# Gates r and z of a graph as one 2 x 2 block product in seven multiplications

## The chip, the cores and the metric

The kernel runs on one NeuronCore of a Trainium2 chip. The core has five engines that each work off their own instruction queue and wait for one another by semaphores: TensorE (PE: matrix multiplications into PSUM; its weight loads, PEld, run beside them), VectorE (DVE), ScalarE (ACT), GpSimd (POOL) and SyncE (SP, which here only issues transfers). All data are float32. The metric is the time of the device in microseconds for one execution of the whole program, median of three runs: 2230.82 us (2230.2 to 2232.75).

## The reference

There are 64 graphs of 256 nodes with 256 features. Layer 0 normalizes the adjacency, multiplies it with the features and a weight and applies a layer norm to the residual sum. Layer 1 computes three things from its result x: a convolution branch `x_conv` (a pointwise convolution, then one with 17 taps along the nodes, with a residual), a message branch `x_nmp`, and a gated recurrent unit that joins them:

```python
x_in = jnp.concatenate([x_conv, x_nmp], axis=-1)
gi = x_in @ w_ih.T + b_ih
gh = x @ w_hh.T + b_hh
r = jax.nn.sigmoid(gi_r + gh_r)
z = jax.nn.sigmoid(gi_z + gh_z)
nn_ = jnp.tanh(gi_n + r * gh_n)
return (1.0 - z) * nn_ + z * x
```

A layer norm follows on x plus this. For r and z the three inputs (x, x_nmp and x_conv, 256 features each) enter one sum, so r and z of a graph are one product of a 256 x 768 matrix with a 768 x 512 matrix, plus a bias. The n gate needs its hidden and its input part apart.

## The kernel before

**Quarters.** The 64 graphs go in four quarters of Q = 16. A quarter passes three stages. *Layer graphs* (`graphs`, which runs `layer0` and `layer1`): per graph the adjacency is transposed, layer 0 computed, x and x_nmp transposed are written to DRAM (`xn_d`, 512 KB a graph), x itself to `x1_d`, and the first half of the convolution's transform goes into the large tile V. *Transform*: the convolution of the whole quarter as a Fourier transform over tiles of nodes: `products` multiplies 71 weight tiles `u` of 256 KB, streamed from DRAM through the ring `ustream`, and `real_transform`, `complex_begin` and `complex_end` do the inverse transform on VectorE, almost all of it with two inputs in SBUF; the result goes to `xc_d`. *Gates* (`gru`, one graph a call).

**How the stages are interleaved.** They are Python generators merged by hand. V shares its memory with the transform's results, so a quarter's graphs and the transform before it exclude one another, except that the first AHEAD = Q // 2 = 8 layer graphs of the next quarter write to a second tile, V2, during the transform; four ScalarE copies then bring V2 into V (L925). The first EARLY = 4 gate graphs of a quarter run among the remaining eight layer graphs of the next; the twelve `late` ones run during that next quarter's transform. A gate graph has four yields; the transform takes 14 of the 48 late yields between its product steps, and the others are merged with `complex_end` and with layer graphs. The last quarter has no graphs behind it: its 16 gate graphs run alone at the end.

**Order.** The tile framework derives all semaphores and gives each engine a fixed order of instructions. This isn't always the program's: an instruction whose buffer or data are there early may stand ahead of one that the program has first.

**A gate graph before.** For each half c of the nodes (128 of 256) TensorE runs six matmuls of 512 columns into one PSUM bank (L748: hidden, x_nmp and xcT terms), the bank `p_rz`, and six of 256 columns into another (L759, `p_n`). In the second half it transposes the convolution of the next graph (`transposed`, L726), from which ScalarE makes `xcT` with bias and ReLU (L728). VectorE adds the bias into `trz` (L763), ScalarE applies tanh with half the argument, which is a sigmoid up to scale (L764), GpSimd computes z3 = z + 3 (L766) and x1 * z3 (L767), VectorE does the n gate (L769, L770, L773), ScalarE its tanh (L776). Both halves done, VectorE joins them (L787, L788), and the layer norm follows: statistics on VectorE (L290 to L292), the power −0.5 on GpSimd (L293), scale on ScalarE (L303), transfer out (L790).

**Loads of the gates.** SP loads `x1_g` (L708), `xn_g` (L710) and the convolution `xc_g` (L704) into rings of two. `residual` (L715) adds x to `xc_g` by an accumulating transfer that GpSimd issues. PSUM has two rings of four banks: `bank` for transposes and layer graphs, `accbank` for products and gates.

**Degrees.** From the third graph on, ScalarE sums the rows of the adjacency with a copy into a tile called `unused` (L324), whose content nobody reads.

Of the kernel before, what the change touches and what calls it, by code (L numbers as in the profile page):

```python
# [9 lines left out]
F32 = mybir.dt.float32  # L10
# [4 lines left out]
P = 128  # L15
# [11 lines left out]
def kernel(  # L27
# [44 lines left out]

    ps = ctx.enter_context(tc.tile_pool(name="ps", bufs=4, space=bass.MemoryType.PSUM))
    psacc = ctx.enter_context(tc.tile_pool(name="psacc", bufs=4, space=bass.MemoryType.PSUM))
    loads = ctx.enter_context(tc.tile_pool(name="loads", bufs=3))
    work = ctx.enter_context(tc.tile_pool(name="work", bufs=2))
    freq = ctx.enter_context(tc.tile_pool(name="freq", bufs=1))
    small = ctx.enter_context(tc.tile_pool(name="small", bufs=4))
# [4 lines left out]
    def accbank(name):  # L83
        return psacc.tile([P, 512], F32, tag="acc", name=name)
# [30 lines left out]

    ident = const.tile([P, P], F32)
    make_identity(nc, ident)
    unused = const.tile([P, N], F32)
    neg_half = const.tile([P, 4], F32)
    nc.vector.memset(neg_half, -0.5)  # L120
    nc.vector.tensor_scalar(alpha_t, alpha_t, MIN_ALPHA, None, op0=ALU.max)
# [7 lines left out]
            nc.gpsimd.memset(t[:, :, c : c + 1], 1.0)  # L129
        scols.append(t)  # L130

    wih = const.tile([P, 2 * DCH, 3 * D], F32)
    whh = const.tile([P, DCH, 3 * D], F32)
    brz_t = const.tile([P, 2 * D], F32)
    bn_t = const.tile([P, 2, D], F32)

    bn2_bias = const.tile([P, DCH], F32)
# [176 lines left out]
    def layer0(g):  # L314

        a_t, x_t = ain.pop(g), xin.pop(g)


        deg = small.tile([P, NCH], F32, name="deg")
        if g < 2:  # L320
            nc.vector.tensor_reduce(deg, a_t, AX.X, ALU.add)
        else:
            for c in range(NCH):
                nc.scalar.activation(unused, a_t[:, c, :], AF.Copy, accum_out=deg[:, c : c + 1])  # L324
        nc.vector.scalar_tensor_tensor(deg, deg, 0.0, deg, op0=ALU.is_equal, op1=ALU.add)
        dis = small.tile([P, NCH], F32, name="dis")
        nc.gpsimd.tensor_tensor(dis, deg, neg_half[:, :NCH], op=ALU.pow)
# [2 lines left out]

        adjT = work.tile([P, NCH, 3, P], F32, name="adjT", bufs=3)
        ADJT[g] = adjT
        p = bank("p_adjT").rearrange("p (c n) -> p c n", c=NCH)
        for mc in range(NCH):
            for c in range(NCH):
# [239 lines left out]
    def turned(re, im, angle):  # L577


        t = freq.tile([P, 2, D], F32, name="turn", bufs=4)  # L580
        x, y = M[:, re, :], M[:, im, :]
        real_part(t[:, int(re > im), :], x, y, angle)
        return imaginary_part(t[:, int(re < im), :], x, y, angle), t
# [4 lines left out]
    def real_transform():  # L588


        sub2(M[:, 0:3:2, :], M[:, 1:4:2, :])
        yield

        sub2(M[:, 4:6, :].rearrange("p a o -> p (a o)"), M[:, 6:8, :].rearrange("p a o -> p (a o)"))
        add2(M[:, 6, :], M[:, 7, :])
        r = math.sqrt(0.5)
        for i, by in enumerate((-1.0, 1.0, -r, r)):
            stt(M[:, 4 + i, :], M[:, 4 + i, :], by, M[:, i, :], op0=ALU.mult, op1=ALU.add)
        stt(M[:, 0:4, :], M[:, 0:4, :], 2.0, M[:, 4:8, :], op0=ALU.mult, op1=ALU.subtract)
        yield  # L600

        four(8, 12)
        yield
        nc.vector.tensor_sub(M[:, 8, :], M[:, 0, :], M[:, 8, :])
        nc.vector.tensor_add(M[:, 12, :], M[:, 4, :], M[:, 12, :])
        for i, x, y in ((1, 9, 13), (2, 10, 14), (3, 15, 11)):
            angle = math.pi * ORDER[i] / 8
            t = freq.tile([P, 2, D], F32, name="turn", bufs=4)
            by = real_part(t[:, 0, :], M[:, x, :], M[:, y, :], angle)
            imaginary_part(t[:, 1, :], M[:, x, :], M[:, y, :], angle)  # L610
            stt(M[:, 8 + i, :], t[:, 0, :], -by, M[:, i, :], op0=ALU.mult, op1=ALU.add)
            stt(M[:, 12 + i, :], t[:, 1, :], by, M[:, 4 + i, :], op0=ALU.mult, op1=ALU.add)
            yield
        stt(M[:, 0:8, :], M[:, 0:8, :], 2.0, M[:, 8:16, :], op0=ALU.mult, op1=ALU.subtract)
        yield
# [39 lines left out]
    def output(q, n, re, im):  # L655


        plain = M[:, n // 8 * 8 + ORDER.index(n % 8), :]
        x, y = M[:, re, :], M[:, im, :]
        t = freq.tile([P, 2, D], F32, name="turn", bufs=4)  # L660
        by = [real_part(t[:, j, :], x, y, 2 * math.pi * (n + 16 * j) / FL) for j in range(2)]
        low = min(re, im)
        for j in range(2):
            stt(M[:, low + 16 * j, :], t[:, j, :], by[j], plain, op0=ALU.mult, op1=ALU.add)  # L664
        nc.sync.dma_start(
            xc_d[q].rearrange("g (t a b) d -> (g t) a b d", a=2, b=16)[:, :, n, :], M[:, low : low + 17 : 16, :]
        )
# [29 lines left out]
            yield  # L697


    GATE, CONV, XCT = {}, {}, {}  # L700

    def load_conv(g):
        CONV[g] = gate.tile([P, NCH, D], F32, name="xc_g")
        nc.sync.dma_start(CONV[g], xc_d[g // Q][g % Q].rearrange("(c p) d -> p c d", p=P))  # L704

    def load_gate(g):
        x1 = gate.tile([P, NCH, D], F32, name="x1_g")
        nc.sync.dma_start(x1, x1_d[g // Q][g % Q].rearrange("(c p) d -> p c d", p=P))  # L708
        xn = gate.tile([P, 2 * DCH, N], F32, name="xn_g")
        nc.sync.dma_start(xn, xn_d[g])  # L710
        GATE[g] = x1, xn

    def residual(g):

# [4 lines left out]
    def transposed(g):  # L719

        xc = CONV.pop(g)
        XCT[g] = gate.tile([P, DCH, N], F32, name="xcT")
        p = bank("p_xcT").rearrange("p (k n) -> p k n", k=DCH)
        for k in range(DCH):
            for c in range(NCH):
                nc.tensor.transpose(p[:, k, c * P : (c + 1) * P], xc[:, c, k * P : (k + 1) * P], ident)  # L726
        for k in range(DCH):
            nc.scalar.activation(XCT[g][:, k], p[:, k], AF.Relu, bias=bn2_bias[:, k : k + 1])  # L728

    def gru(g):  # L730

        following = g % Q + 1 < Q
        (x1, xn), xcT = GATE.pop(g), XCT.pop(g)
        trz = gate.tile([P, NCH, 2 * D], F32, name="trz", bufs=1)
        nn = gate.tile([P, NCH, D], F32, name="nn", bufs=1)
        if following:
            load_gate(g + 1)
        for c in range(NCH):
            cs = slice(c * P, (c + 1) * P)

            hid = [(xn[:, k, cs], whh[:, k, :]) for k in range(DCH)]
            inp = [(xn[:, DCH + k, cs], wih[:, DCH + k, :]) for k in range(DCH)]
            inp += [(xcT[:, k, cs], wih[:, k, :]) for k in range(DCH)]

            q = accbank("p_rz")
            terms = hid + inp
            for j, (lhsT, w) in enumerate(terms):
                nc.tensor.matmul(q, lhsT, w[:, : 2 * D], start=j == 0, stop=j == len(terms) - 1)  # L748
            if following and c == 1:
                transposed(g + 1)  # L750
            yield
            if following and c == 0:
                residual(g + 1)
            if c == 1 and g % Q + 2 < Q:
                load_conv(g + 2)
            p = accbank("p_n")
            for o, terms in ((1, hid), (0, inp)):
                for j, (lhsT, w) in enumerate(terms):
                    nc.tensor.matmul(  # L759
                        p[:, o * D : (o + 1) * D], lhsT, w[:, 2 * D :], start=j == 0, stop=j == len(terms) - 1  # L760
                    )

            nc.vector.tensor_add(trz[:, c, :], q, brz_t)  # L763
            nc.scalar.activation(trz[:, c, :], trz[:, c, :], AF.Tanh, scale=0.5)  # L764
            z3 = gate.tile([P, D], F32, name="z3", bufs=1)
            nc.gpsimd.tensor_scalar(z3, trz[:, c, D:], 3.0, None, op0=ALU.add)  # L766
            nc.gpsimd.tensor_tensor(x1[:, c, :], x1[:, c, :], z3, op=ALU.mult)  # L767
            gn = gate.tile([P, 2, D], F32, name="gn")
            nc.vector.tensor_add(gn, p.rearrange("p (i d) -> p i d", i=2), bn_t)  # L769
            nc.vector.scalar_tensor_tensor(  # L770
                gn[:, 1, :], trz[:, c, :D], 1.0, gn[:, 1, :], op0=ALU.add, op1=ALU.mult
            )
            nc.vector.scalar_tensor_tensor(  # L773
                gn[:, 0, :], gn[:, 1, :], 0.5, gn[:, 0, :], op0=ALU.mult, op1=ALU.add
# [8 lines left out]
            else:  # L783
                yield
                continue
            y, t, n = x1[:, part], trz[:, part, D:], nn[:, part]
            nc.vector.scalar_tensor_tensor(n, t, 1.0, n, op0=ALU.subtract, op1=ALU.mult)  # L787
            nc.vector.tensor_sub(y, y, n)  # L788
            layernorm(y, nc.scalar, 4 * LN_EPS)
# [48 lines left out]
    with tc.tile_pool(name="setup", bufs=1) as setup:  # L838
# [8 lines left out]
        load(2)  # L847

        def gate_weights():
            nc.sync.dma_start(whh, w_hhT.rearrange("(k p) o -> p k o", p=P))  # L850
            nc.sync.dma_start(wih, w_ihT.rearrange("(k p) o -> p k o", p=P))
            yield

        others = [weights(setup, i, Q, scale2) for i in range(Q)]
        others[4] = chain(others[4], gate_weights())
        run(graphs(0, range(Q), V, others))
        bih_t = setup.tile([P, 3 * D], F32, name="bih", tag="taps", bufs=2)
        nc.sync.dma_start(bih_t, bcast_rows(b_ih, 3 * D))
        bhh_t = setup.tile([P, 3 * D], F32, name="bhh", tag="taps", bufs=2)
        nc.sync.dma_start(bhh_t, bcast_rows(b_hh, 3 * D))  # L860
        nc.vector.tensor_add(brz_t, bih_t[:, : 2 * D], bhh_t[:, : 2 * D])
        nc.vector.tensor_copy(bn_t[:, 0, :], bih_t[:, 2 * D :])
        nc.vector.tensor_copy(bn_t[:, 1, :], bhh_t[:, 2 * D :])
    ustream = ctx.enter_context(tc.tile_pool(name="ustream", bufs=6))
    gate = ctx.enter_context(tc.tile_pool(name="gate", bufs=2))
    ahead = ctx.enter_context(tc.tile_pool(name="ahead", bufs=1))


    AHEAD = Q // 2
    V2 = ahead.tile([P, FL, DCH, AHEAD * GT], F32, name="V2")  # L870
    EARLY = 4

    def gates(q, part):

        for i in part:
            if i == 0:
# [4 lines left out]
                residual(q * Q)  # L881
                yield
                transposed(q * Q)
                yield
            yield from gru(q * Q + i)

# [99 lines left out]
```

## Time and profile before

| what | value |
|---|---|
| median of three runs | 2230.82 us (2230.2 to 2232.75) |
| profiled execution | 2229.6 us |
| its span, first to last instruction | 2227.7 us |
| TensorE clock granted, mean | 0.993 |
| VectorE, ScalarE, GpSimd busy | 1347.2, 839.9, 611.9 us |
| L748, three groups of 512 records | 243.2, 243.0, 241.3 us busy |
| L759, three groups of 512 records | 133.2, 131.7, 131.4 us busy |
| last transform: first product, last store to `xc_d` | 1708.0, 1913.5 us |

A logical float32 matmul shows as two records. The busy mean of a TensorE record (593 ns for 512 columns) overlaps its neighbours, since matmuls are pipelined; the distance from one to the next is the price, and the chain of waits gives it. Busy times of the other engines are of single instructions, which also overlap a little when they follow one another without a wait. Where a line gives a releaser ("<-ACT trz L764 649.9"), the engine sat idle that long until the named instruction was done.

### The profile page before, as it was taken

What the parts mean: (1) busy time and instruction counts of PE and PEld (TensorE: products, weight loads), DVE (VectorE), ACT (ScalarE), POOL (GpSimd) and SP (SyncE); (2) the same over time, 40 slices, a digit from 0 to 9 for tenths busy, and PEclk for the clock granted to TensorE, in tenths of its full rate; (3) what the DMA queues carried; (4) which work ended last, traced back from release to release, by engine and by line L of the source; (5) the groups of instructions that cost most, each with busy time, mean ns of one, the idle gap of its engine ahead of it and who ended that gap; (6) DMA issues with size and microseconds to landing.
All of it is one profiled execution on the core that took longest, in us unless ns stands there. A gap on an engine that the chain in (4) does not pass through costs nothing. (4 is left out here: it accounts for less than half of the span.)

```text
span 2227.7 us, 26520 instructions
## 1 busy us (share of the span) xinstructions
PE 2140.2 (96%) x8701; PEld 1533.4 (69%) x8701; DVE 1347.2 (60%) x3487; ACT 839.9 (38%) x1850; POOL 611.9 (27%) x656
## 2 busy tenths in 40 slices
PE   5999989999999999999999999999999999999998
PEld 4777768777767766777667766777776765556555
DVE  6555558895447796545446779545444779644444
ACT  3565633456431124446441122555532112222222
POOL 2344320113211133222221133222221114433332
PEclk9999999999999999999999999999999999999999
DMA  4655667444346644333236655333324655433331
GB/s 121 199 173 158 182 219 235 156 144 125 105 128 194 187 136 136 113 95 111 79 102 181 196 165 146 100 109 109 100 76 128 198 157 141 124 100 99 100 99 52
DMA packets 249732, 305.03 MB, mean 137 GB/s; under 512 B 18458, under 2 KB 227626, under 8 KB 249595
## 3 DMA queue, kind: packets, MB, share of 16 engines
q1 hardware_dynamic: 181500, 199.85, 29.2%
q10 hardware_dynamic: 45280, 68.04, 8.4%
q0 software_dynamic: 22816, 35.45, 8.3%
q8 instruction: 69, 1.13, 0.2%
q14 instruction: 67, 0.55, 0.1%
HBM read 200.71 MB, written 102.57 MB: 136 GB/s over the span
## 5 line engine op out<-in xcount | busy, mean ns | idle before, releaser
L766 POOL TENSOR_SCALAR z<-trz 128x256 f32<-128x256 f32 x128 | 125.0, 977 | 649.9 <-ACT trz L764 649.9
L748 PE MATMUL p_rz<-wih,xcT 128*128 128x512 f32 x512 | 241.3, 593 | 2.2 <-ACT xcT L728 2.2
L748 PE MATMUL p_rz<-wih,xn_g 128*128 128x512 f32 x512 | 243.2, 594 | 0.0
L748 PE MATMUL p_rz<-whh,xn_g 128*128 128x512 f32 x512 | 243.0, 594 | 0.0
L293 POOL TENSOR_TENSOR ln_rs<-ln_rs,neg_half 128x2 f32<-128x2 f32 x129 | 99.0, 767 | 428.9 <-DVE ln_rs L292 371.7
L763 DVE TENSOR_TENSOR trz<-p_rz,brz_t 128x512 f32<-128x512 f32 x128 | 87.7, 686 | 164.5 <-PE p_rz L748 164.4
L776 ACT ACTIVATE nn<-gn 128x256 f32<-128x256 f32 x128 | 53.3, 417 | 351.6 <-DVE gn L773 351.1
L748 PEld LDWEIGHTS p_rz<-wih,xcT 128*128 128x128 f32 x512 | 96.9, 190 | 124.0 <-issue 120.2
L748 PEld LDWEIGHTS p_rz<-wih,xn_g 128*128 128x128 f32 x512 | 96.2, 190 | 118.3 <-issue 118.2
L486 PE MATMUL p_k<-u,VM 128*128 128x256 f32 x736 | 175.2, 380 | 0.8 <-DMA u<-ud 0.7
L769 DVE TENSOR_TENSOR gn<-p_n,bn_t 128x512 f32<-128x512 f32 x128 | 88.1, 688 | 143.3 <-PE p_n L759 143.2
L486 PEld LDWEIGHTS p_k<-u,VM 128*128 128x128 f32 x736 | 138.3, 190 | 24.9 <-issue 4.6
L358 PE MATMUL p_hT<-adjT,x 128*128 128x256 f32 x512 | 126.9, 393 | 19.4 <-DVE adjT L341 11.9
L748 PEld LDWEIGHTS p_rz<-whh,xn_g 128*128 128x128 f32 x512 | 94.6, 190 | 64.8 <-issue 59.6
L303 ACT ACTIVATE x_g<-x_g,ln_mr,ln_rs 128x256 f32<-128x256 f32 x128 | 70.0, 593 | 181.4 <-DVE ln_mr L301 181.4
L764 ACT ACTIVATE trz<-trz 128x512 f32<-128x512 f32 x128 | 80.5, 629 | 152.8 <-DVE trz L763 108.3
L396 PE MATMUL p_conv<-wc,xn 128*128 128x259 f32 x512 | 126.9, 390 | 7.5 <-ACT xn L388 7.5
L759 PE MATMUL p_n<-whh,xn_g 128*128 128x256 f32 x512 | 133.2, 383 | 0.0
L759 PE MATMUL p_n<-wih,xn_g 128*128 128x256 f32 x512 | 131.7, 379 | 0.0
L759 PE MATMUL p_n<-wih,xcT 128*128 128x256 f32 x512 | 131.4, 379 | 0.0
L431 PE MATMUL p_dft<-fwd,h 128*128 128x240 f32 x512 | 117.9, 374 | 13.7 <-ACT h L400 13.3
L462 PE MATMUL p_nmp<-aT,msg 128*128 128x256 f32 x512 | 123.6, 385 | 5.9 <-DVE aT L457 5.9
(149 smaller groups left out, 4123.8 us busy)
## 6 DMA issues: line engine op xcount, KB each, us to landing
u<-ud SPq DMA_DIRECT2D x284, 256.0 KB
xn_d<-xn ACTq DMA_DIRECT2D x64, 512.0 KB
xn_g<-xn_d SPq DMA_DIRECT2D x64, 512.0 KB
adj_t<-in_adj_dram SPq DMA_DIRECT2D x64, 256.0 KB
x_t<-in_x_dram SPq DMA_DIRECT2D x64, 256.0 KB
x_d<-x ACTq DMA_DIRECT2D x64, 256.0 KB
x_g<-x_d SPq DMA_DIRECT2D x64, 256.0 KB
xc_d<-VM SPq DMA_DIRECT2D x64, 256.0 KB
```

Of the source, the lines that this page charges most:

```text
L293: nc.gpsimd.tensor_tensor(rs[:, : len(chunks)], rs[:, : len(chunks)], neg_half[:, : len(chunks)], op=ALU.pow)
L358: nc.tensor.matmul(p[:, k, :], x1[:, mc, k * P : (k + 1) * P], adjT[:, mc, 1 - mc : 3 - mc, :].rearrange("p n q -> p (n q)"), start=mc == ...
L396: nc.tensor.matmul(p, x1T[:, k, c * P : (c + 1) * P], wc1[:, k, :], start=k == 0, stop=k == DCH - 1)
L431: nc.tensor.matmul(p[:, t0 * FL : t1 * FL], h[:, c, k * P : (k + 1) * P], fwd[:, first : first + t1 - t0, :].rearrange("p t f -> p (t f)") ...
L462: nc.tensor.matmul(p[:, k, :], msg[:, mc, k * P : (k + 1) * P], aT[:, mc].rearrange("p n q -> p (n q)"), start=mc == 0, stop=mc == NCH - 1,)
L486: nc.tensor.matmul(p[:, j * D : (j + 1) * D], v[:, k, :], u[:, k, :], start=k == 0, stop=k == DCH - 1)
L748: nc.tensor.matmul(q, lhsT, w[:, : 2 * D], start=j == 0, stop=j == len(terms) - 1)
L759: nc.tensor.matmul(p[:, o * D : (o + 1) * D], lhsT, w[:, 2 * D :], start=j == 0, stop=j == len(terms) - 1)
L763: nc.vector.tensor_add(trz[:, c, :], q, brz_t)
L764: nc.scalar.activation(trz[:, c, :], trz[:, c, :], AF.Tanh, scale=0.5)
L766: nc.gpsimd.tensor_scalar(z3, trz[:, c, D:], 3.0, None, op0=ALU.add)
L769: nc.vector.tensor_add(gn, p.rearrange("p (i d) -> p i d", i=2), bn_t)
```

## The change

Write a graph's inputs, transposed and stacked (768 rows: x, x_nmp, xcT; HALF = 3 of its six row blocks each), as a 2 x 2 block matrix: the halves of the nodes against the halves of the inputs. The weights of r and z form one too: halves of the inputs against the columns of r and of z. The product of two such block matrices takes eight block products; in Strassen's form (Winograd's variant) it takes seven, with sums of blocks ahead and behind. The change does this:

- `gate_weights` loads three weight blocks and one for the sums (B11, B21, B22, T1), and makes the sums T1 to T4 by four VectorE subtractions, once. The weights of n get their own tile `wn`. It is now spread over graphs 4 to 6 of the first quarter.
- `input_sums` makes four sums of input blocks a graph, 128 x 384 each, on GpSimd, called for the next graph during a graph's n gate. x, x_nmp and xcT now share one tile, `inputs`.
- `gru` runs seven block products of three matmuls of 256 columns into four PSUM banks (the last half of one is empty), and five VectorE and GpSimd operations put r and z together: `first` (the first product plus bias), then `trz` in three VectorE additions that read PSUM, and one on GpSimd, 512 columns wide, that adds `first` to both z parts. The bias of z is stored less that of r. Two tanh of 512 columns follow, for r and for z. The transposes of the next graph come ahead of the n gate.
- Buffers: rings of loads 3 to 2, `turn` 4 to 3, `xc_g` 2 to 1, `ustream` 6 to 5, the tile `unused` goes (the copy of the degrees writes into `adjT`, which is filled later), V2 holds AHEAD = 6 graphs, and EARLY is 5, so that 44 late yields are left.

```diff
-    loads = ctx.enter_context(tc.tile_pool(name="loads", bufs=3))
+    loads = ctx.enter_context(tc.tile_pool(name="loads", bufs=2))
...
-                nc.scalar.activation(unused, a_t[:, c, :], AF.Copy, accum_out=deg[:, c : c + 1])
+                nc.scalar.activation(adjT[:, c, 0:2, :].rearrange("p n q -> p (n q)"), a_t[:, c, :], AF.Copy, accum_out=deg[:, c : c + 1])
...
-        CONV[g] = gate.tile([P, NCH, D], F32, name="xc_g")
+        CONV[g] = gate.tile([P, NCH, D], F32, name="xc_g", bufs=1)
...
+    def halves(inputs):
+
+        return [inputs[:, i * HALF : (i + 1) * HALF, c * P : (c + 1) * P] for c in range(2) for i in range(2)]
+
+    def input_sums(g):
+        A11, A12, A21, A22 = halves(GATE[g][1])
+        S = SUMS[g] = gate.tile([P, 4, HALF, P], F32, name="sums", bufs=1)
+        nc.gpsimd.tensor_tensor(S[:, 2], A11, A21, op=ALU.subtract)
+        nc.gpsimd.tensor_tensor(S[:, 0], A21, A22, op=ALU.add)
+        nc.gpsimd.tensor_tensor(S[:, 1], S[:, 0], A11, op=ALU.subtract)
+        nc.gpsimd.tensor_tensor(S[:, 3], A12, S[:, 1], op=ALU.subtract)
...
-            q = accbank("p_rz")
-            terms = hid + inp
-            for j, (lhsT, w) in enumerate(terms):
-                nc.tensor.matmul(q, lhsT, w[:, : 2 * D], start=j == 0, stop=j == len(terms) - 1)
-            if following and c == 1:
-                transposed(g + 1)
-            yield
-            if following and c == 0:
-                residual(g + 1)
...
+        def block(p, j, a, b):
+            for k in range(HALF):
+                nc.tensor.matmul(
+                    p[:, j * D : (j + 1) * D], a[:, k], wrz[:, b, k], start=k == 0, stop=k == HALF - 1
+                )
+
+        p15, p26 = accbank("p_rz"), accbank("p_rz")
+        block(p15, 0, A11, B11)
+        block(p26, 0, A12, B21)
+        block(p15, 1, S[:, 0], T1)
+        block(p26, 1, S[:, 1], T2)
+        yield
+        if following:
+            residual(g + 1)
+        first = gate.tile([P, 2, D], F32, name="first", bufs=1)
+        nc.vector.tensor_add(first, half(p15), brz_t)
+        nc.vector.tensor_add(trz[:, 0:2], first[:, 0:1].to_broadcast([P, 2, D]), half(p26))
+        p7, p34 = accbank("p_rz"), accbank("p_rz")
+        block(p7, 0, S[:, 2], T3)
+        block(p34, 0, S[:, 3], B22)
+        block(p34, 1, A22, T4)
+        nc.vector.tensor_add(trz[:, 3], trz[:, 1], p7[:, :D])
+        nc.vector.tensor_add(trz[:, 1:3], trz[:, 1:4:2], half(p34))
+        nc.gpsimd.tensor_tensor(
+            trz[:, 1:4:2], trz[:, 1:4:2], first[:, 1:2].to_broadcast([P, 2, D]), op=ALU.add
+        )
+
+        for i in range(2):
+            nc.scalar.activation(trz[:, i:4:2], trz[:, i:4:2], AF.Tanh, scale=0.5)
+        if following:
+            transposed(g + 1)
+        yield
         for c in range(NCH):
...
+            if c == 0 and following:
+                input_sums(g + 1)
             if c == 1 and g % Q + 2 < Q:
                 load_conv(g + 2)
...
-            nc.vector.tensor_add(trz[:, c, :], q, brz_t)
-            nc.scalar.activation(trz[:, c, :], trz[:, c, :], AF.Tanh, scale=0.5)
...
-    ustream = ctx.enter_context(tc.tile_pool(name="ustream", bufs=6))
+    ustream = ctx.enter_context(tc.tile_pool(name="ustream", bufs=5))
...
-    AHEAD = Q // 2
+    AHEAD = 6
...
-    EARLY = 4
+    EARLY = 5
```

## The prediction

> **What bounds the kernel now.** I read the page's busy shares first, then the groups of instructions, then the chain that ended last, then busy times by stretch, then single instructions on GpSimd. The shares:
>
> ```profile
> PE 2140.2 (96%) x8701; PEld 1533.4 (69%) x8701; DVE 1347.2 (60%) x3487; ACT 839.9 (38%) x1850; POOL 611.9 (27%) x656
> PE   5999989999999999999999999999999999999998
> ```
>
> TensorE is busy in every slice after the first. The chain of waits prices the gates (windowed to 1800–1970 us; columns: start, length, piece):
>
> ```profile
> 1909.25 5.15 PE p_rz L748 x12
> 1914.40 0.44 PE p_xcT L726 x4
> 1914.84 2.59 PE p_n L759 x12
> 1917.43 5.15 PE p_rz L748 x12
> ```
>
> Twelve 128x512 records take 5.15 us (0.429 each), twelve 128x256 records 2.59 us (0.2158 each): time goes with the columns, and a narrow matmul loses nothing although each has its own weight load. A logical matmul is two records. A gate graph is 2 x (5.15 + 2.59) + 0.44 = 15.92 us, and the pure gate stretch at the end repeats at exactly that. The stretches:
>
> ```profile
> 400.00:502.00 102.00, 94.98 (x441) 73.05 (x439) 90.22 (x257) 51.85 (x117) 17.47 (x17) 1.00 0.45 145
> 1298.00:1386.00 88.00, 87.68 (x303) 54.13 (x301) 83.63 (x211) 22.69 (x50) 30.27 (x28) 1.00 0.49 140
> 1825.00:1914.00 89.00, 86.81 (x283) 51.50 (x282) 83.42 (x199) 18.07 (x37) 38.65 (x27) 1.00 0.45 127
> 1965.00:2220.00 255.00, 254.46 (x830) 151.65 (x828) 115.06 (x263) 63.27 (x129) 82.45 (x96) 1.00 0.35 92
> ```
>
> Columns after the length: busy us of PE, weight loads, DVE, ACT, POOL. In the last stretch (gates alone) only TensorE is full; DVE is at 45%, GpSimd at 32%. But where the inverse transform is merged with gates (1298–1386, 1825–1914, and 767–856 with 84.35 of 89), DVE is at 94–95%. Work taken from TensorE there is worth nothing once DVE is the longer one. GpSimd in such a stretch:
>
> ```profile
> 1888.92 2.57 POOL L766 TENSOR_SCALAR z<-trz 128x256 f32<-128x256 f32 x1 [7.08 <-ACT trz L764]
> 1891.58 3.87 POOL L767 TENSOR_TENSOR x_g<-x_g,z 128x256 f32<-128x256 f32 x1
> ```
>
> and over the whole run (ns, least/median/most):
>
> ```profile
> L351 POOL TENSOR_TENSOR x_t<-x_t,b_t x64: 1256/1268/1737, 11.9 to 1647.6; 128x512 f32<-128x512 f32 x64
> L767 POOL TENSOR_TENSOR x_g<-x_g,z x128: 713/727/3866, 528.2 to 2219.4; 128x256 f32<-128x256 f32 x128
> ```
>
> The same multiplication takes 0.73 us alone and up to 3.87 beside a full DVE.
>
> **What the Trainium skill says.** "GPSIMD Engine Reference", section 3.1: a two-input elementwise operation costs GpSimd about 2.6 cycles of 1.2 GHz an element (2.17 ns). The trace agrees: (1256 − 713)/256 = 2.12 ns, plus 0.17 us fixed. "SBUF — State Buffer", section "Who interferes with whom": a VectorE instruction with two SBUF inputs contends with a GpSimd instruction that reads SBUF, one input (the other in PSUM) does not. The trace agrees on the blocking: at 1891.58 the multiplication lasts 3.87 us beside two-input transform steps; at 1862.55 it runs in 0.72 and a transform step (L574) beside it takes 0.94 instead of 0.42. "Trainium Kernel Development and Optimization", "Key Constraints": GpSimd can't access PSUM; so DVE must do the additions that read products, and only one of the recombinations can go to GpSimd. No row here tests that.
>
> **The change part by part.**
>
> *TensorE, removed:* per graph 24 records of 512 columns, 10.30 us. *Added:* seven products of three matmuls, 42 records of 256 columns x 0.2158 = 9.06. Saving 1.24 us a graph, x 64 = **−79.2 us**. A gate graph becomes 14.68. Nothing else on TensorE changes in amount.
>
> *DVE, added:* per graph two L763 additions (0.69 each) become first, trz 0:2 and trz 1:3 at 512 columns and one at 256: 3 x 0.69 + 0.42 = 2.49 against 1.38; in back-to-back flow, where the timeline spaces 512-wide ones 0.60 and 256-wide ones 0.335 apart, 2.14 against 1.21. About +1 us a graph. In the last stretch DVE goes from 7.2 to 8.3 us of 14.68: hidden by the products.
>
> *GpSimd, added:* four sums of 384 columns, 0.17 + 384 x 0.00212 = 0.98 each, and the z addition of 512 columns, 1.26: +5.2 us a graph. Before: two z (0.855), two x_g (0.73), ln_rs 0.72, residual's transfer 1.26 = 5.15. After 10.3 of 14.68: not the bound by its sum. ACT: two tanh of 512 columns as before; the second waits for GpSimd.
>
> *The three merged stretches:* 44 records of each of three L748 kinds in 1825–1914, eight of each a graph, are 5.5 graphs. Ideal length 89 − 5.5 x 1.24 = 82. DVE would need 83.4 + 5.5 x 0.93 = 88.5, and each added GpSimd operation holds a two-input DVE step about 0.4 us (0.94 against 0.42 above; 0.83 against 0.42 at 1911.75): 27 x 0.4 = 11 at most, 99 in all. Between 89 and 99, some transform work sliding into later stretches that have room (in 1386–1542 DVE is at 78.5 of 156): I take 92, so 10 us back each, **+30** (bounds +15 to +50).
>
> *The moved graphs:* AHEAD 8 to 6. A layer graph is 12.2 us of TensorE: 32 records x 0.216, 8 of conv x 0.218, 8 of the transform x 0.2, 4 of dist x 0.216, 10 transposes x 0.11. In the first round there are no gates to fill with, and 400–502 has DVE at 90 of 102: moving two graphs out takes 24.4 us from TensorE but only about 13 from DVE (7.4 busy a graph, less overlap). I take half of the difference back, **+6** (0 to +12). In later rounds one gate graph moves from late to early: late 12 to 11 graphs. The last round's transform then has 11 x 14.68 us of gates as cover where it had 12 x 15.92, 30 us less; gates of the round begin at about 1965 while DVE ends the transform at 1914 and the reload, residual, transposes and sums take some 15 us: a slack of 36. Still hidden, with about 6 to spare; if DVE is 20 late, 14 are lost (inside the bound above).
>
> *Rings.* u 6 to 5: one buffer is four records, 0.86 us less lead; TensorE waited 5 us for u in all. loads 3 to 2: a load starts one graph later, still one layer graph (over 12 us) ahead. xc_g 2 to 1: the reload of g+2 starts after the transposes of g+1; 3 us reload (2058.14 to the residual's issue at 2061.32), 1.26 issue, 4.4 landing = 9 of 14.68. GpSimd's sums, z, x_g and ln_rs queue behind a residual that waits for a late reload; SP's other loads stand behind the reload's own wait. Together **+3** (0 to +15). Weight loads: as many bytes in more transfers, and four subtractions of 768 columns (0.95 each by the 512 and 1024 rows) in the first stage, DVE at 26 of 50: nothing; uncovered 4. Degrees written into adjT: its third buffer was last read a graph before: nothing; uncovered, 0.4 a graph. *Layer norms behind the sums:* ln_rs and dis queue on GpSimd behind up to 4 us of sums, and DVE's L301 waits in order, with transform and PSUM readings behind it: **+6** in the three graph stages, **+3** in the last stretch (0 to +25).
>
> Sum: −79.2 + 30 + 6 + 3 + 9 = −31. The profiled execution took 2229.6 us (span 2227.7 and 1.9 around it): 2198.4. The median of the runs is 1.2 higher: **2199.6**.
>
> **Rivals.** (1) *Near the full saving*: DVE's ending transform slides and GpSimd's waits stay local. For it: DVE averages 60%, TensorE's waits are a few us. Against: 94% in three stretches. −79 + 25 = −54 or better: 2150–2177. (2) *Slower, by a ring through GpSimd in gru.* In the program's order: z addition 1.26, tanh 0.63, two xcT 0.84, four sums 3.94, z and x_g twice with gaps 3.46, L788 to ln_rs 2.1 (timeline), ln_rs 0.72, residual 1.26, hand-offs 0.4: 14.6 us, as long as TensorE's 14.68. It decides from 15.92: with the mean excess of z and x_g over quiet (0.977 and 0.878 against 0.855 and 0.727, about 0.14) on eleven operations it is 16.1: the 47.5 graphs outside the merged stretches lose 0.2 each, 10 us. Inside, the means are 1.57 and 1.72, 0.85 in excess; if half of the eleven meet it, the ring is 19.3, and 16.5 graphs lose 3.4 each, 56 us. Doubled inputs and x1 let TensorE run a graph ahead of the ring, so I take half of the 66: 2264 (2240 to 2297). Against it: the queue isn't in program order (a residual at 2061.32 stands ahead of the ln_rs at 2065.68 of a graph before), S, z3 and the additions only need their own data. (3) *No net change*: the merged stretches become DVE's, 3 x 18, and the ring costs 25: 2231.
>
> **How the numbers follow.** Two runs differ by up to 0.1%, so 0.2% (4.5 us) is about what tells from no change. Partial saving (2177–2218) 0.38, near full 0.20, about nothing (2218–2240) 0.10, slower 0.32, nearly all the ring. Faster: 0.58 and 0.03 of the third: 0.61; same 0.06; slower 0.33. Range 2158 to 2260: it leaves 0.06 below and 0.14 above; the likeliest case alone is 2177–2218.
>
> **What would show it.** 42 p_rz records a graph, 256 columns each and 0.216 apart; the last stretch at 14.7 a graph; no TensorE wait on the sums tile. DVE at 97% in the merged stretches, GpSimd near 945 us busy plus blocking. Wrong if TensorE waits for sums, xc_g or p_rz readings in the last stretch, or if the DVE-full stretches grow by more than 10 us each.

## The result and the profile after

The changed kernel takes 2328.7 us (median of four runs, 2323.78 to 2333.23) against 2231.78 for the kernel before beside it: ratio 1.0434, interval 1.041 to 1.0458. It is 4.3% slower. The forecast was 1.4% faster, and the time lies 69 us above the range.

The page's shares, profiled execution of the changed kernel (span 2325.4 us):

```profile
PE 2115.7 (91%) x9853; PEld 1771.3 (76%) x9853; DVE 1543.1 (66%) x3620; ACT 839.1 (36%) x1850; POOL 971.1 (42%) x976
PE   5999989979899997999899998799999999789998
```

TensorE is no longer full; VectorE has 196 us more than before, GpSimd 359 more. The chain of waits, end of the span:

```profile
2094.82 9.06 PE p_rz L759 x42
2104.48 5.18 PE p_n L798 x24
2109.66 9.06 PE p_rz L759 x42
```

TensorE's own sum came out to the digit: 42 records in 9.06 us. A graph takes 14.84 us here, against 15.92 before. Busy times by stretch (columns after the length as above: PE, weight loads, DVE, ACT, POOL, then the granted clock). The first runs from just before the last product of the third quarter to the first of the last four stores of its transform (1490.1), the second is the pure gate stretch:

```profile
1371.00:1490.00 119.00, 98.40 (x438) 81.51 (x437) 113.56 (x237) 28.86 (x60) 66.81 (x59) 0.95 0.45 124
2094.00:2300.00 206.00, 205.95 (x979) 179.88 (x978) 144.27 (x252) 54.74 (x112) 159.02 (x155) 1.00 0.41 107
```

From the last product to the very last store (1372.6 to 1497.1), this merged stretch now takes 124.5 us; before, it took 88.8. The other two went from 88.8 and 89.3 us to 123.9 and 129.3. TensorE has work for 98 of the 119 us shown, and VectorE is nearly full. The stretch isn't the same work as before, though: up to the last store VectorE has 252 instructions in it instead of 211, since it now also takes in the added gate operations and more of the next layer graphs. Single instructions in it, first GpSimd, then VectorE:

```profile
1398.75 3.39 POOL L780 TENSOR_TENSOR trz<-trz,first 128x512 f32<-128x512 f32 x1 [2.71 <-DVE trz L779]
1402.11 1.18 POOL L741 TENSOR_TENSOR sums<-inputs 128x384 f32<-128x384 f32 x1
1403.37 1.05 POOL L742 TENSOR_TENSOR sums<-sums,inputs 128x384 f32<-128x384 f32 x1
1404.50 1.06 POOL L743 TENSOR_TENSOR sums<-inputs,sums 128x384 f32<-128x384 f32 x1
```

```profile
1400.94 0.68 DVE L806 TENSOR_TENSOR gn<-p_n,bn_t 128x512 f32<-128x512 f32 x1
1402.35 1.21 DVE L807 SCALAR_TENSOR_TENSOR gn<-trz,gn 128x256 f32<-128x256 f32 x1
1403.49 1.21 DVE L567 SCALAR_TENSOR_TENSOR turn<-VM 128x256 f32<-128x256 f32 x1
1404.62 1.22 DVE L810 SCALAR_TENSOR_TENSOR gn<-gn 128x256 f32<-128x256 f32 x1
```

Here the two engines step in turn: each 256-wide VectorE instruction with both inputs in SBUF lasts 1.21 us instead of 0.41 to 0.42, one to a sum. L806, which reads PSUM, keeps its 0.68. Just before, it is GpSimd that is held: the z addition (L780) takes 3.39 us instead of 1.26. These lines are the extreme, not the rule: of the 96 transform steps of 256 columns in the stretch, 11 last over 1 us (2 in the kernel without sums, below). TensorE's longest totals of waiting:

```profile
PE p_dft L434 <- ACT h L403: 80.5, 31, 9.6
PE p_rz L759 <- POOL sums L741: 22.0, 12, 2.5
PE p_k L489 <- DMA u<-ud: 16.1, 19, 2.1
```

Only 22 us is a wait for the sums themselves. The wait for h (L403) is 80.5 us here and 13.3 before. The eight parts of the span, cut at each transform's first product and at each copy into V, add to the 97.7 us between the two spans. Times in us of the profiled executions:

| part | before | changed | by TensorE's work alone |
|---|---|---|---|
| start to first product | 310.2 | 318.5 | 0 |
| first transform, to the copy into V | 183.4 | 178.4 | −24.4 |
| graphs, second quarter | 158.3 | 202.9 | +34.1 |
| second transform with gates | 359.7 | 343.8 | −54 |
| graphs, third quarter | 170.5 | 213.5 | +34.1 |
| third transform with gates | 360.3 | 342.7 | −54 |
| graphs, fourth quarter | 165.6 | 213.3 | +34.1 |
| fourth transform and gates to the end | 519.7 | 512.3 | −49.4 |

The last column is the change that the two moved layer graphs (12.2 us each), the moved gate graph and the 1.24 us saved a graph would make. What each part lost against it: 8.3, 19.4, 10.5, 38.1, 8.9, 36.4, 13.6 and 42.0, together 177. The three parts in which transform and gates run together hold 116 of it.

### The profile page after: what moved, and what is told of

It reads as the page before. It is cut to its first block, busy times and chain, and to the rows that moved or that the text cites. A ratio compares the mean times of both kernels' runs of the same rounds, so it can differ in the third digit from the quotient of the medians.

```text
span 2325.4 us, 29417 instructions
## 1 busy us (share of the span) xinstructions
PE 2115.7 (91%) x9853; PEld 1771.3 (76%) x9853; DVE 1543.1 (66%) x3620; ACT 839.1 (36%) x1850; POOL 971.1 (42%) x976
## 5 line engine op out<-in xcount | busy, mean ns | idle before, releaser
L759 PE MATMUL p_rz<-wrz,sums 128*128 128x256 f32 x1536 | 363.7, 388 | 34.2 <-POOL sums L741 22.0
L759 PEld LDWEIGHTS p_rz<-wrz,sums 128*128 128x128 f32 x1536 | 292.4, 193 | 90.8 <-POOL sums L741 26.9
L798 PE MATMUL p_n<-wn,inputs 128*128 128x256 f32 x1536 | 355.6, 385 | 6.0 <-DVE first L772 5.8
L798 PEld LDWEIGHTS p_n<-wn,inputs 128*128 128x128 f32 x1536 | 289.6, 193 | 51.6 <-DVE first L772 8.0
L759 PE MATMUL p_rz<-wrz,inputs 128*128 128x256 f32 x1152 | 273.6, 381 | 2.9 <-ACT inputs L731 2.9
L759 PEld LDWEIGHTS p_rz<-wrz,inputs 128*128 128x128 f32 x1152 | 217.9, 191 | 33.7 <-ACT inputs L731 4.6
L434 PE MATMUL p_dft<-fwd,h 128*128 128x240 f32 x512 | 141.3, 428 | 80.6 <-ACT h L403 80.5
L434 PEld LDWEIGHTS p_dft<-fwd,h 128*128 128x128 f32 x512 | 109.7, 221 | 106.1 <-ACT h L403 95.6
L740 POOL TENSOR_TENSOR sums<-inputs 128x384 f32<-128x384 f32 x64 | 66.8, 1044 | 219.2 <-issue 172.3
L354 POOL TENSOR_TENSOR x_t<-x_t,b_t 128x512 f32<-128x512 f32 x64 | 87.6, 1370 | 128.0 <-ACT x L353 105.2
L806 DVE TENSOR_TENSOR gn<-p_n,bn_t 128x512 f32<-128x512 f32 x128 | 87.6, 684 | 61.3 <-PE p_n L798 60.5
L306 ACT ACTIVATE x<-x,ln_mr,ln_rs 128x256 f32<-128x256 f32 x128 | 70.3, 595 | 157.7 <-DVE ln_mr L304 157.6
```

The costliest lines, as they stand in the source:

```text
L306: nc.scalar.activation(y[:, c, :], y[:, c, :], AF.Identity, bias=mr[:, c : c + 1], scale=rs[:, c : c + 1])
L354: nc.gpsimd.tensor_tensor(x_t, x_t, b0_t.unsqueeze(1).to_broadcast([P, NCH, D]), op=ALU.add)
L434: nc.tensor.matmul(p[:, t0 * FL : t1 * FL], h[:, c, k * P : (k + 1) * P], fwd[:, first : first + t1 - t0, :].rearrange("p t f -> p (t f)") ...
L740: nc.gpsimd.tensor_tensor(S[:, 2], A11, A21, op=ALU.subtract)
L759: nc.tensor.matmul(p[:, j * D : (j + 1) * D], a[:, k], wrz[:, b, k], start=k == 0, stop=k == HALF - 1)
L798: nc.tensor.matmul(p[:, o * D : (o + 1) * D], lhsT, w, start=j == 0, stop=j == len(part) - 1)
```

## The experiments

Three theories were set up. A: GpSimd's added operations, which read SBUF, shut out VectorE's instructions with two SBUF inputs. B: what makes room costs (rings, moved graphs, the degrees). C: GpSimd's time and queue cost, because others wait behind it. Times are medians in us, each beside the kernel before as measured with it (2232.17 for the first four experiments, 2229.63 and 2231.31 for the others).

**Smaller rings alone.**

```diff
-    loads = ctx.enter_context(tc.tile_pool(name="loads", bufs=3))
+    loads = ctx.enter_context(tc.tile_pool(name="loads", bufs=2))
...
-        CONV[g] = gate.tile([P, NCH, D], F32, name="xc_g")
+        CONV[g] = gate.tile([P, NCH, D], F32, name="xc_g", bufs=1)
...
-    ustream = ctx.enter_context(tc.tile_pool(name="ustream", bufs=6))
+    ustream = ctx.enter_context(tc.tile_pool(name="ustream", bufs=5))
```

(and `turn` 4 to 3)

> The kernel before with the smaller rings alone: loads 3 to 2, turn 4 to 3, xc_g 2 to 1, ustream 6 to 5. Theory A (GpSimd's added operations hold VectorE up in the merged stretches and that is nearly all of the loss): within 6 us of the kernel before, as in the prediction's sum (+3, 0 to +15). Theory B (the room made is what costs): 20 to 50 us slower, with TensorE waiting for u, xc_g and x_t.

Measured: 2255.85, ratio 1.0101 (1.0077 to 1.0125), +23.7 us against 2232.17. TensorE's wait for u in the profile:

```profile
PE p_k L486 <- DMA u<-ud: 16.3, 17, 2.8
```

It was 3.3 us before. Theory A's 6 us is wrong here; the rings cost four times that, which lies in theory B's range.

**Degrees into adjT alone.**

```diff
-                nc.scalar.activation(unused, a_t[:, c, :], AF.Copy, accum_out=deg[:, c : c + 1])
+                nc.scalar.activation(adjT[:, c, 0:2, :].rearrange("p n q -> p (n q)"), a_t[:, c, :], AF.Copy, accum_out=deg[:, c : c + 1])
```

> The kernel before with the degrees' copy written into adjT instead of a tile that nobody reads, nothing else. Theory A: no change (0 to +3 us). Theory B: +8 us in the first 310 us of the span, where the changed kernel has no gates yet and loses 8.5 us, and about 6 us in each later stretch of layer graphs, 20 to 35 us in all, with TensorE waiting for h (L400) as in the changed kernel (80 us there, 13 before).

Measured: 2228.96, ratio 0.9988 (0.9979 to 0.9996): it costs nothing. The first product comes at 315.6 instead of 310.2, but later parts give this back. TensorE waits 21.4 us for h here, so this edit alone doesn't explain the 80 us of the changed kernel. (Without its sums, below, that wait is 50.3 us.)

**Moved graphs alone.**

```diff
-    AHEAD = Q // 2
+    AHEAD = 6
...
-    EARLY = 4
+    EARLY = 5
```

> The kernel before with AHEAD 6 and EARLY 5 alone. Theory A: +6 us, all of it in the first quarter's transform, where VectorE is the longer one (0 to +12, the prediction's bounds). Theory B (the moved graphs are the cover that the transforms miss): +40 us or more, 10 to 15 in each of the four transforms.

Measured: 2249.42, ratio 1.0074 (1.0047 to 1.01), +17.2. By parts the first transform is 9.5 us shorter instead of 24.4, so 15 are lost there, where the prediction had placed them, but more than its bound of 12; the other transforms are shorter by 39.7 and 41.6 for 40.3 of work taken out. The place was right, the size was not; theory B's loss in all four transforms isn't there.

**No sums of inputs** (products read blocks of inputs).

```diff
-        S = SUMS[g] = gate.tile([P, 4, HALF, P], F32, name="sums", bufs=1)
-        nc.gpsimd.tensor_tensor(S[:, 2], A11, A21, op=ALU.subtract)
-        nc.gpsimd.tensor_tensor(S[:, 0], A21, A22, op=ALU.add)
-        nc.gpsimd.tensor_tensor(S[:, 1], S[:, 0], A11, op=ALU.subtract)
-        nc.gpsimd.tensor_tensor(S[:, 3], A12, S[:, 1], op=ALU.subtract)
+        SUMS[g] = (A21, A22, A11, A12)
```

> The changed kernel without its four sums of inputs a graph: the products that read sums read input blocks instead, so r and z of every graph are other numbers; all else stays. Theory A: the merged stretches lose most of their growth; four of the five added GpSimd operations are gone, so 80 to 110 us faster than the changed kernel (2220 to 2250), VectorE busy 1440 instead of 1543. Theory B: at most 30 us faster (2300 or more), since rings, degrees and moved graphs stay as they are.

Measured: 2229.45, ratio to the kernel before 0.9986 (0.9975 to 0.9998): 99 us faster than the changed kernel, as theory A said. VectorE busy went from 1543.1 to 1449.0 us. The second to fourth transforms went from 343.8 to 322.9, from 342.7 to 322.4, and from 512.3 to 486.5. The merged stretch of the third quarter between the same marks as above (first of the last four stores):

```profile
1331.00:1437.00 106.00, 94.00 (x437) 80.02 (x436) 100.66 (x237) 28.82 (x61) 45.55 (x39) 0.98 0.48 139
```

With the same 237 VectorE instructions it takes 106 us instead of 119, and VectorE is busy 100.7 us instead of 113.6: 20 sums in it hold VectorE 0.65 us each. But without any sum it is still far above the 92 us of the forecast. The sums are the whole of what the change loses against the kernel before; but not of what it lost against the forecast, since without any sums it still only ties.

**Fills instead of sums.** The question is whether GpSimd's reading costs, or its time.

```diff
-        nc.gpsimd.tensor_tensor(S[:, 2], A11, A21, op=ALU.subtract)
-        nc.gpsimd.tensor_tensor(S[:, 0], A21, A22, op=ALU.add)
-        nc.gpsimd.tensor_tensor(S[:, 1], S[:, 0], A11, op=ALU.subtract)
-        nc.gpsimd.tensor_tensor(S[:, 3], A12, S[:, 1], op=ALU.subtract)
+        for i in (2, 2, 0, 0, 1, 1, 3, 3):
+            nc.gpsimd.memset(S[:, i], 0.5)
```

> The changed kernel with each of its four input sums replaced by two GpSimd fills of the same tile (384 columns; about 0.42 us each by the fills of 2 and 256 columns at 0.094 and 0.31, 3.3 us a graph against 3.9 of quiet sums). GpSimd writes but reads nothing from SBUF; TensorE still waits for the tile. The inputs' sums are left out, so r and z are other numbers. Theory A (GpSimd's reads shut out VectorE's instructions with two SBUF inputs): near the kernel without sums, 2230 to 2250, and the VectorE rows in the merged stretches back at 0.42 us. Theory C (it is GpSimd's time and its queue that TensorE, the layer norms and VectorE wait for): near the changed kernel, 2300 or more.

Measured: 2242.5, ratio 1.0061 (1.0046 to 1.0076): 13 above the kernel without sums, 86 below the changed kernel. The fills took 0.418 us each; GpSimd is busy 871.2 us, against 688.2 without sums and 971.1 with them. The merged stretch of the third quarter is 108 us, again to the first of the last four stores:

```profile
1340.00:1448.00 108.00, 93.72 (x438) 80.29 (x437) 102.08 (x236) 28.76 (x60) 59.31 (x79) 0.97 0.47 138
```

VectorE's transform steps in that stretch (columns at the end: count, busy us, mean ns of one, idle time before), changed kernel:

```profile
L567 DVE SCALAR_TENSOR_TENSOR turn<-VM 128x256 f32<-128x256 f32 x22 | 10.7, 489 | 0.0
L569 DVE SCALAR_TENSOR_TENSOR turn<-VM 128x256 f32<-128x256 f32 x14 | 8.6, 622 | 0.0
L538 DVE TENSOR_TENSOR VM<-VM 128x512 f32<-128x512 f32 (+2 forms) x7 | 7.5, 1075 | 0.0
```

and with fills:

```profile
L567 DVE SCALAR_TENSOR_TENSOR turn<-VM 128x256 f32<-128x256 f32 x21 | 8.6, 416 | 0.0
L569 DVE SCALAR_TENSOR_TENSOR turn<-VM 128x256 f32<-128x256 f32 x14 | 6.7, 493 | 0.0
L538 DVE TENSOR_TENSOR VM<-VM 128x512 f32<-128x512 f32 (+2 forms) x7 | 5.9, 837 | 0.0
```

Two thirds of GpSimd's added time kept (183 of 283 us), and with it TensorE's wait on the tile, brings back an eighth of the loss (13 of 99). The fills don't wait for the inputs as the sums do and are shorter, so this bounds theory C rather than measures it; the parts of the span, below, show where it holds. What remains of L569 and L538 above 0.42 and 0.69 is from the GpSimd operations that stay: without any sums they are at 0.506 and 0.838.

**Sums on VectorE.** (`nc.gpsimd` to `nc.vector` in the four lines.)

> The changed kernel with the four sums on VectorE, all of the computation done. Theory A: VectorE does them in 4 x 0.46 us a graph (384 columns between 0.335 and 0.605), 118 us of work instead of the 94 us of it that the sums on GpSimd cost it as blocking (1543 against 1449 busy), and the queue on GpSimd is short again: between 15 us slower and 45 us faster than the changed kernel, 2285 to 2345. Theory C: 60 us faster or more, 2270 or less.

Measured: 2266.18, ratio 1.017 (1.0154 to 1.0185): 62 us faster than the changed kernel, more than either end that theory A gave, and what theory C had said (60 or more). Theory A's number took all of VectorE's work as lost. VectorE is busy 1573.2 us, 30 more than in the changed kernel, and yet the end is earlier.

**Where the sums cost.** The parts of the profiled spans show it. The table has differences to the kernel without sums, in us, for the changed kernel and for the fills; in each part VectorE has as many instructions as without sums, or one more or less.

| part | sums: time | sums: VectorE busy | fills: time |
|---|---|---|---|
| start to the first copy into V | −3.6 | +0.6 | −1.4 |
| product steps of the three later transforms | −1.8 | +14.4 | −3.6 |
| their merged stretches, last product to last store | +45.5 | +47.4 | +1.6 |
| from there to the copy into V, second and third | +16.5 | −0.8 | +5.6 |
| three stages of layer graphs | +36.2 | +1.8 | +15.1 |
| from the last store of the fourth to the end | +6.9 | +30.7 | −0.7 |

So theories A and C both hold, each in its place. In the merged stretches VectorE is full, the sums hold it 47 us longer on the same instructions (0.71 for each of 67 sums), and the time grows by as much; fills, which read nothing, cost almost nothing there. That is theory A, with about half of the 99 us. In the two parts with layer graphs VectorE is about half idle and not held longer, so its hold can't be what costs 53 us. Fills cost 21 there, and sums on VectorE, out of GpSimd's queue, cost 5 in the three stages of layer graphs instead of 36. That is theory C. VectorE's wait for the layer norm's power on GpSimd (`ln_mr` for `ln_rs`) in these three stages is 81.5 us with the sums, 68.4 with fills, 59.4 without either and 50.2 with the sums on VectorE. How the 53 us divide between GpSimd's time, its waiting for inputs and the lower clock that TensorE had there (0.958, 0.976 and 0.976 in the three stages, against 0.982, 1.0 and 1.0 without sums), no run separates.

**No added GpSimd operation at all.**

```diff
-        nc.gpsimd.tensor_tensor(
+        nc.vector.tensor_tensor(
             trz[:, 1:4:2], trz[:, 1:4:2], first[:, 1:2].to_broadcast([P, 2, D]), op=ALU.add
```

(and no sums, as above)

> The changed kernel without the sums (products read input blocks, r and z are other numbers) and with the addition to the z parts on VectorE, so that GpSimd has no operation that the kernel before did not have. Theory A (that addition, 512 columns with two SBUF inputs, shuts VectorE out like a sum): VectorE gains 0.6 us a graph but loses the blocking and the hand-over to GpSimd, 8 to 25 us faster than without the sums alone (2229.45): 2204 to 2221. If the rest of the loss lies elsewhere (rings, cover, VectorE's own additions): 2222 to 2240.

Measured: 2215.46, ratio 0.993 (0.9916 to 0.9945): 14 below the kernel without sums. So each of the 64 z additions cost 0.22 us more on GpSimd than on VectorE, which got their work here. With no added GpSimd operation at all, the three merged stretches still last 113.8, 114.1 and 115.3 us to the last store.

**The weight ring alone** (`ustream` 6 to 5).

> The kernel before with ustream 6 to 5 alone. All four smaller rings together cost 22.6 us there (2255.85 against 2232.17 at the medians) and TensorE's wait for u rose from 3.3 to 16.3 us. If the weight ring is what costs: 11 to 18 us slower. If x_t's or xc_g's ring is: under 5 us.

Measured: 2244.36, ratio 1.007 (1.0053 to 1.0088), +14.7 us. Waits of TensorE:

```profile
PE p_k L486 <- DMA u<-ud: 14.0, 22, 1.5
```

The weight ring is about two thirds of the rings' cost. How the rest is split between x_t, xc_g and turn wasn't tried. (All four rings cost 23.7 us by the medians; the 22.6 of the expectation fits the ratio times the median, not their difference.)

**All that makes room, no seven products.**

> The kernel before with all that makes room: the four smaller rings, AHEAD 6 and EARLY 5, the degrees into adjT; no seven products. One by one against the kernel before they gave +22.6, +16.5 and -2.7 us (differences of medians). If they add: 2264 to 2272. If they get in each other's way (the shorter weight ring hurts more where fewer layer graphs cover): 2275 to 2300. If they overlap: 2245 to 2260.

Measured: 2265.85, ratio 1.0154 (1.014 to 1.0168), +34.5, in the range for parts that add. By the medians the parts were +23.7, +17.2 and −3.2 (the expectation's figures again fit the ratios), together 37.7, which is 34.5 to within what the runs scatter.

**Seven products where no transform runs.** The kernel before with all its rings, and the seven products in the last quarter's 16 gate graphs alone; their weights, sums and `first` lie in V2, which is free by then.

```diff
+            prepare()
             run(gates(q, range(Q)))
...
-            yield from gru(q * Q + i)
+            yield from (gru7 if q == NQ - 1 else gru)(q * Q + i)
...
+    def input_sums(g):
+        A11, A12, A21, A22 = halves(GATE[g][1])
+        S = spare()[1]
+        nc.gpsimd.tensor_tensor(S[:, 2], A11, A21, op=ALU.subtract)
...
```

(`gru7` is the changed kernel's `gru`; `spare` gives views of V2; `prepare` makes the weight sums once, on VectorE.)

> The kernel before, all its rings, AHEAD and EARLY as they were, with the seven products in the last quarter's 16 gate graphs alone, where no transform runs beside them (their weights, sums and first lie in V2, which is free by then). All of the computation done. Theory A: a graph there at 14.7 to 14.9 us instead of 15.92, as the changed kernel shows, so 15 to 19 us faster than the kernel before: 2213 to 2217. Theory B or C: no such gain, since GpSimd's queue is as long there: 2225 or more.

Measured: 2213.2, ratio 0.9927 (0.9913 to 0.9941), 16.4 us faster than the kernel before: 1.03 a graph. The chain at its start:

```profile
1965.75 9.07 PE p_rz L847 x42
1974.82 0.44 PE p_xcT L727 x4
1975.26 5.18 PE p_n L885 x24
1980.44 9.06 PE p_rz L847 x42
```

A graph is 14.69 us, with the sums on GpSimd. VectorE is slowed there too; this group is of the changed kernel, in its gate stretch 2094 to 2300:

```profile
L810 DVE SCALAR_TENSOR_TENSOR gn<-gn 128x256 f32<-128x256 f32 x28 | 30.6, 1093 | 1.0
```

1.09 us each, where the same step took 0.43 in the gate stretch before, and TensorE is full all the same: VectorE has the room, busy 144 of 206 us. With the sums on VectorE in this kernel:

> The kernel with the seven products in the last quarter alone, the sums on VectorE. VectorE is at about 70% there with the sums on GpSimd in the changed kernel. Theory A: the stretch is TensorE's in both, so within 3 us of the kernel with the sums on GpSimd: 2209 to 2217. If GpSimd's sums still cost something there: 2205 to 2209.

Measured: 2213.66, ratio 0.9924 (0.9911 to 0.9937): no difference, as theory A said. Both beat the kernel before and the changed one.

## Why the prediction was wrong

The sum was −79.2 of TensorE and +48 given back. The runs, each against the kernel before as measured with it, give: room +34.5; seven products without any added GpSimd operation −50 (2215.46 against 2265.85); the z addition on GpSimd +14; the four sums on GpSimd +99. Together +97, which is the result.

- *TensorE, −79.2*: right where nothing else binds: 42 records in 9.06, 14.69 to 14.84 a gate graph. Over the whole kernel 50 of 79 arrive even with no added operation on GpSimd; by parts, the second and third transform are only 6.6 and 3.9 us shorter than with the room alone, for 13.6 of work removed. So the +30 that the prediction gave back in the merged stretches was about used up before GpSimd did anything more. That VectorE's own additions hold these 29 is argued from its load (1472 us busy against 1355); no run separates it.
- *The price of GpSimd's added operations*: **this is the step that failed.** The prediction gave them 3.5 us in each merged stretch (92 instead of 88.5) and 9 for layer norms behind the sums, about 20 us in all. They cost 113. The hold in the merged stretches was put at 0.4 us an operation, "11 at most", and most of that was to slide into later stretches. The sums alone made them 12.3, 13.2 and 20.0 us longer, 0.71 us of VectorE's time each, and nothing slid away: the stretches have the same VectorE instructions with and without sums. "About 0.4" came from GpSimd operations that stood singly; several in a row before a full queue of VectorE cost more, as the lines from 1402 on show.
- *Layer norms behind the sums, +9 (0 to 25)*: the other half of the same step. The stages of layer graphs lost 33 us against their work (10.5, 8.9, 13.6), and 36 of the 99 us that the sums cost lie in them (202.9, 213.5 and 213.3 against 188.9, 203.4 and 201.1 without sums), with 16 more where layer graphs run behind the second and third transform. The mechanism is seen in VectorE's wait for `ln_rs`, which grew by 22 us in the three stages; the size was beyond the bound.
- *The merged stretches at 92 us each*: they took 124.5, 123.9 and 129.3 to the last store, and 109 to 112 without any sum. "DVE would need 88.5" counted the stretch's old work and the gates' additions; in the changed kernel it takes in more (252 VectorE instructions for 211), so its length against the kernel before doesn't tell what was lost. The parts of the span do.
- *"GpSimd 10.3 of 14.68, not the bound by its sum"*: true, and where the gates run alone it was all that mattered (14.84 us a graph, although GpSimd's 10.3 and VectorE's 8.3 together are more than that). It says nothing of what these operations take from VectorE where VectorE is full, nor of what waits behind them.
- *Moved graphs, +6 (0 to 12)*: right place, wrong size: 15 in the first transform, +17.2 in all. Even the whole difference between TensorE's 24.4 and VectorE's 13, of which the prediction took half, is less than that.
- *Rings, +3 (0 to 15)*: +23.7. The prediction took TensorE's small wait for u as a sign of spare lead. One buffer less raised the wait by 11 us and the time by 14.7.
- *Degrees, nothing*: right.
- *The slower rival* had the sign (0.32), not the mechanism: its ring through GpSimd would have made 16.1 us of a graph where the gates run alone, and it was 14.84. In all, TensorE waited 22 us for sums.

## What to carry to other kernels

Price an operation moved to GpSimd twice: at what its reading of SBUF takes from VectorE's steps with two SBUF inputs, where VectorE is full, and at what stands behind it in GpSimd's queue. Here 256 sums of about 1 us cost 99 us, half of it in the first way and half in the second, among layer graphs where VectorE was half idle. Only in the gates alone, where TensorE was the one full engine, were they free. Take work from the full engine stage by stage; the same seven products, with what makes room for them, lose 4.3% over the whole kernel and gain 0.7% in the one stage where TensorE alone is full. A ring that was never waited for long may still have nothing to spare, and moved work costs where the cover was thinnest.

## What the runs showed of the hardware that was not expected

From 1402 to 1406 us three GpSimd sums and three two-input instructions of VectorE alternate one for one, 1.13 us from one VectorE start to the next. That is less than a quiet sum (0.99) and a quiet VectorE step (0.34 from start to start) one after the other, so they don't shut each other out for their whole length. The hold goes both ways: before that, at 1398.75, a VectorE at its full pace stretched the z addition to 3.39 us. A GpSimd fill of the same tile does little of this: VectorE is busy 19 us longer with 512 fills, 94 with 256 sums.

A starved TensorE went with a lower granted clock. Over 1371 to 1490, where it had work for 98 of 119 us, the clock was 0.95, over 1400 to 1450 (42 of 50) it was 0.93, and over 2094 to 2300, where it was full, 1.00; the kernel's mean fell from 0.993 to 0.974. With the sums TensorE is busy 34 us longer than without for the same 9853 records (2115.7 against 2081.5); how much of that is the clock isn't separated.
